# Softmax row sums over DMAs in place of VectorE turns, and a second pair of blocks joined, in a four-layer graph network on one core

## The chip, the core and the metric

The kernel runs on one core of a Trainium2 chip. The metric is the device time of one execution in microseconds, lower is better. The core has five engines that run their own instruction streams in order: TensorE (PE; its weight loads are PEld), VectorE (DVE), ScalarE (ACT), GpSimd (POOL) and SyncE (SP), which here only issues DMAs.

## What is computed

The input x holds 32 batches of 512 nodes with 64 features, adj is one 512 x 512 matrix. Each of four layers normalises x over its features, applies relu, and adds what a graph layer makes of it. Layers 0 to 2 take the first fifth of the time (the first `top_row` of layer 3 is issued at 464.4 us), and the change doesn't touch them. Layer 3, which the change is in, is a graph attention with eight heads and an output layer that is an attention of the same kind:

```
def gat_layer(x, graph, W, b):
    h = x @ W
    s = jnp.einsum('bnd,bmd->bnm', h, h) * graph
    s = jnp.where(s == 0.0, NEG_INF, s)
    a = jax.nn.softmax(s, axis=2)
    return jnp.einsum('bnm,bmd->bnd', a, h) + b
heads = jax.vmap(lambda W, b: gat_layer(flow_x, graph, W, b))(Wh, bh)
H, B, N, D = heads.shape
cat = jnp.moveaxis(heads, 0, 2).reshape(B, N, H * D)
x = jax.nn.leaky_relu(cat, negative_slope=0.01)
out = gat_layer(x, graph, W_out, b_out)
return jax.nn.leaky_relu(out, negative_slope=0.01)
```

So for each batch and head there is a 512 x 512 table of scores, an exp of it less the row's maximum, a sum of each row, a product of the exps with the values, and a division of that product by the row sums. All of it is fp32.

## The kernel before

**Units.** Layer 3 is cut into 144 units. A unit is a pair of attentions: two heads of one batch (class Heads, four units a batch), or the output layer of two batches (class Out). N = 512 is cut into C = 4 blocks of 128 rows (r, or j in the products), and a tile of a unit holds one block for both members of the pair, 128 x 1024. After eight units of heads comes one of Out, so the work repeats every nine units. Out follows the heads that it needs at a distance (LATE, line 305).

**The steps of a unit, by name and line (of the kernel before).**
- scores(r), L368: two matmuls into a PSUM tile `s_ps` of the pool `ps_s`, which has two buffers of two banks each.
- maxima(r), L380: VectorE reads `s_ps`, adds the mask, writes `p_att` to SBUF and leaves the row's extreme in `top`, once for each member of the pair.
- spread_out, L387 and L390: VectorE turns `top` in 32 x 32 blocks into `top_t`, and four DMAs write it to DRAM. spread_in, L396: one DMA reads it back, repeated over all 128 partitions, as `topb`.
- shift(r), L402: GpSimd subtracts `topb` from `p_att`.
- exps(r), L411: ScalarE's exp, in place; for r = 2 it goes to PSUM instead, into a tile `e_ps` that takes a buffer of `ps_s`.
- join, L414: VectorE adds block 1 to the `e_ps` of block 2 and writes the sum where block 2 was. Block 1 itself stays.
- totals, L435 and L443: TensorE sums over partitions with a matrix of ones into four groups of 32 rows of `tot_ps`: block 0 and the joined block over all 512 columns, and then block 3 in two halves of 256 columns. Then VectorE turns `tot_ps` (L450), and ScalarE gathers the first column of each block in five small copies (L453, L455) into `parts`.
- values(j), L422: the product with the values, in `av`, a PSUM tile with one buffer. Since the joined block holds e1 + e2 and is multiplied by v2, block 1 is multiplied by v1 - v2 (`hd` of L514, `gD` of L618), so that e1 v1 + e2 v2 comes out.
- recips, L461, L464 and L466: add the parts, take the reciprocal, turn it back over all partitions (`recb`).
- normalize, L473: `o_att` = `av` times `recb`.
- y_pe, y_act, y_dve (L555, L565, L573): the bias and leaky relu of heads, in `cat`. product (L601): the output layer's product with `wo_sb`, for odd batches. For Out: back, back_dve, back_pool and store.
- g (L537, copied by L549), hx (L298) and `gV` (L614) prepare later units.

**Their order.** No scheduler reorders this stage: the function planned writes out one period by hand, and each engine runs its instructions in the order in which they stand there. unit(k) in period t is the unit that began k periods ago, so one period works on units at different steps. Before the change, a unit has its scores and maxima 0 and 1 in period -1, 2 and 3 and the spread in period 0, the shifts, exps and the join in period 1, totals, values, recips and normalize in period 2, and y or back in period 3. VectorE's order in a period is: maxima 2 and 3, `top_t`, cat, maxima 0 and 1 of the next unit, `tot_t`, join, recips, normalize. SyncE's order is `top_row`, `topb` and, after an Out, the two stores of `out_dram`.

## Time and profile before

| | us |
|---|---|
| runs of the kernel before, median of 3 | 2138.51 |
| their lowest and highest | 2137.26, 2145.68 |
| the profiled execution | 2142.56 |
| its span, first to last instruction | 2140.8 |
| TensorE's granted clock in it | 0.986 of full speed |
| maxima on VectorE (L380), 1152 of them | 724.5 |
| shifts on GpSimd (L402), 576 | 1348.7 |
| turns of the totals (L450), 144 | 102.2 |
| small copies of `parts` (L455), 576 | 124.1 |

A group of the profile is one line, engine and form: its count, the busy time of all of them, the mean of one in nanoseconds, and then the idle time of its engine just ahead of it with what ended that. A timeline line is start, duration, engine, line, operation, output and inputs; where several instructions follow each other they are merged and their number stands last, and the idle time before them is in brackets. A window line is a stretch of the span, its length, and how long each engine was busy in it. Busy times of neighbours overlap a little[...], so where a length matters it is read from start to start.

### The profile page before, as it was taken

The numbers are of one execution on the slowest core, as the hardware profiler recorded it, in microseconds if no ns is written. First come the engines' busy times: TensorE is split into PE (matmuls) and PEld (weight loads), VectorE is DVE, ScalarE is ACT, GpSimd is POOL, SyncE is SP. The second block draws the span as 40 slices with busy tenths as digits, with TensorE's granted clock in tenths as the row PEclk, the third lists the DMA queues.
The fourth block names the chain that finished last, engine by engine and source line by source line (L and its number), as shares of the span: only waits on it lengthen the run. The fifth ranks groups of instructions, "written<-read, shape, count | busy, mean of one in ns | idle before, by whom it ended". The sixth has DMA issues, their size and how long they took to land.

```text
span 2140.8 us, 34626 instructions
## 1 busy us (share of the span) xinstructions
PE 2056.7 (96%) x12190; PEld 841.5 (39%) x12190; DVE 1825.7 (85%) x4401; ACT 1293.7 (60%) x2520; POOL 1428.5 (67%) x697
## 2 busy tenths in 40 slices
PE   7999999989999999999999999999999999999996
PEld 4667676643333333333333333333333333333332
DVE  6699997669888989898889889888988898888994
ACT  3444443337666767676666666766666676766654
POOL 3000000028888878888888888888887887878896
PEclk9999999979999999999999999999999999999998
DMA  5000000001111111111111111111111111111112
GB/s 137 1 1 1 1 2 1 2 21 50 41 50 54 42 55 51 45 50 55 41 55 55 41 55 51 45 50 55 41 55 50 41 50 41 50 50 42 49 50 52
DMA packets 54567, 89.90 MB, mean 42 GB/s; under 512 B 30008, under 2 KB 35296, under 8 KB 54256
## 3 DMA queue, kind: packets, MB, share of 16 engines
q1 hardware_dynamic: 53872, 87.39, 12.5%
q8 instruction: 98, 1.61, 0.3%
q0 software_dynamic: 512, 0.20, 0.1%
q14 instruction: 85, 0.70, 0.1%
HBM read 81.73 MB, written 4.78 MB: 40 GB/s over the span
## 4 chain that ended last, share of the span: by engine, by line
PE 61%; DVE 22%; ACT 7%; POOL 4%; issue 3%; DMA 3%; SPq 0%; DVEq 0%; POOLq 0%; ACTq 0%
PE av L422 17%; DVE p_att L380 13%; PE s_ps L368 9%; PE nt_ps L876 8%; PE acc L968 6%; PE gT_ps L601 5%; PE tot_ps L435 5%; POOL p_att L402 4%; PE g_ps L537 3%; DVE cat L573 2%; PE tot_ps L443 2%; DMA topb<-top_row 2%; ACT parts L455 1%; PE po L895 1%; ACT p_att L411 1%
## 5 line engine op out<-in xcount | busy, mean ns | idle before, releaser
L402 POOL TENSOR_TENSOR p_att<-p_att,topb 128x1024 f32<-128x1024 f32 x576 | 1348.7, 2376 | 280.7 <-DMA topb<-top_row 114.8
L380 DVE CUSTOM_DVE_ANT_0 p_att<-s_ps,flow_neg 128x512 f32<-128x512 f32 x1152 | 724.5, 684 | 120.6 <-PE s_ps L368 120.2
L368 PE MATMUL s_ps<-hx,g 64*128 64x512 f32 x2048 | 529.9, 615 | 25.7 <-DVE p_att L414 6.9
L411 ACT ACTIVATE p_att<-p_att 128x1024 f32<-128x1024 f32 x432 | 456.5, 1057 | 97.5 <-POOL p_att L402 89.4
L422 PE MATMUL av<-p_att,hn 128*64 128x512 f32 x1536 | 379.5, 601 | 0.0
L368 PEld LDWEIGHTS s_ps<-hx,g 64*128 64x128 f32 x2048 | 174.3, 186 | 334.3 <-DVE top L380 189.0
L411 ACT ACTIVATE e_ps<-p_att 128x1024 f32<-128x1024 f32 x144 | 148.0, 1028 | 172.5 <-DVE top L380 124.9
L1044 POOL TENSOR_TENSOR x<-x,bias_b 128x512 f32<-128x512 f32 x16 | 20.3, 1273 | 283.4 <-DVE hn L818 283.4
L573 DVE SCALAR_TENSOR_TENSOR cat<-y_ps,bh,cat 128x512 f32<-128x512 f32 x256 | 177.4, 734 | 16.9 <-ACT cat L565 13.0
L565 ACT ACTIVATE cat<-y_ps,bh 128x512 f32<-128x512 f32 x256 | 160.8, 679 | 33.0 <-PE y_ps L555 32.6
L414 DVE TENSOR_TENSOR p_att<-e_ps,p_att 128x1024 f32<-128x1024 f32 x144 | 170.7, 1185 | 7.5 <-ACT e_ps L411 7.5
L422 PEld LDWEIGHTS av<-p_att,hn 128*64 128x64 f32 x1536 | 98.8, 136 | 198.9 <-issue 198.9
L435 PE MATMUL tot_ps<-p_att,ones 128*32 128x512 f32 x1152 | 155.6, 612 | 10.4 <-DVE cat L573 9.5
L555 PE MATMUL y_ps<-o_att,wh_sb 64*128 64x512 f32 x512 | 133.3, 597 | 4.0 <-DVE o_att L473 4.0
L422 PE MATMUL av<-p_att,hd 128*64 128x512 f32 x512 | 131.6, 592 | 0.0
L455 ACT COPY parts<-tot_t 32x16 f32<-32x16 f32 x576 | 124.1, 215 | 6.7
L549 ACT COPY g<-g_ps 128x512 f32<-128x512 f32 x128 | 68.7, 589 | 95.7 <-PE g_ps L537 95.7
L968 PE MATMUL acc<-v,s 64*128 64x65 f32 x2048 | 123.8, 279 | 0.7 <-DVE s L954 0.4
L968 PEld LDWEIGHTS acc<-v,s 64*128 64x128 f32 x2048 | 120.8, 194 | 5.9 <-DVE o L984 1.2
L601 PE MATMUL gT_ps<-cat,wo_sb 128*64 128x512 f32 x512 | 120.7, 592 | 0.0
L876 PE MATMUL nt_ps<-adj_t,hn 128*128 128x512 f32 x256 | 119.2, 610 | 0.8 <-DVE hn L840 0.8
L450 DVE STREAM_TRANSPOSE tot_t<-tot_ps 128x512 f32<-128x512 f32 x144 | 102.2, 710 | 19.1 <-PE tot_ps L443 19.0
(186 smaller groups left out, 2291.8 us busy)
## 6 DMA issues: line engine op xcount, KB each, us to landing
topb<-top_row SPq DMA_DIRECT2D x144, 512.0 KB
top_row<-top_t SPq DMA_DIRECT2D x576, 1.0 KB
out_dram<-y SPq DMA_DIRECT2D x32, 128.0 KB
x<-in_x_dram SPq DMA_DIRECT2D x3, 1024.0 KB
x<-in_x_dram SPq DMA_DIRECT2D x4, 256.0 KB
adj_raw<-in_adj_dram SPq DMA_DIRECT2D x1, 1024.0 KB
mask<-mask SPq DMA_DIRECT2D x4, 256.0 KB
wh_sb<-in_L_gnn_Wh_dram SPq DMA_DIRECT2D x2, 256.0 KB
```

The lines of the kernel that those rows point to most:

```text
L368: nc.tensor.matmul(ps[:, k], lhsT=g[halves(k), r * P : (r + 1) * P], rhs=x[halves(k), :], start=True, stop=True,)
L380: nc.vector.tensor_tensor_reduce(out=self.p[r][:, k], in0=ps[:, k], in1=flow_neg[:, r], scale=-1.0, scalar=BIG, op0=OP.add, op1=OP.min, ac ...
L402: nc.gpsimd.tensor_tensor(self.p[r], self.p[r], self.topb, OP.subtract)
L411: nc.scalar.activation(to, self.p[r], AF.Exp, scale=-1.0)
L414: nc.vector.tensor_tensor(self.p[JOIN + 1], self.joined, self.p[JOIN], OP.add)
L422: nc.tensor.matmul(self.av[halves(k), :], lhsT=self.less_next(k) if j == JOIN else self.v(k, j), rhs=self.p[j][:, k], start=(j == 0), stop ...
L435: nc.tensor.matmul(ps[q : q + 32, :], lhsT=ones, rhs=self.p[j][:, k], start=True, stop=False,)
L565: nc.scalar.activation(self.cat[:, k], self.y[k], AF.Identity, bias=bh01[:, h : h + 1], scale=0.01)
L573: nc.vector.scalar_tensor_tensor(self.cat[:, k], self.y[k], bh[:, h : h + 1], self.cat[:, k], op0=OP.add, op1=OP.max,)
L601: nc.tensor.matmul(self.gps[halves(k), :], lhsT=wo_sb[:, h, :], rhs=Heads.cat.pop((self.b + k, h)), start=(h == 0), stop=(h == H - 1),)
L876: nc.tensor.matmul(p, lhsT=lhs(k), rhs=adj_t[:, k, :], start=(k == 0), stop=(k == C - 1))
L968: nc.tensor.matmul(self.acc[k][:, r], lhsT=self.s[b // 2][halves(k), b % 2, r * P : (r + 1) * P], rhs=self.v[halves(k), b], start=(b == 0) ...
```

## The change

It does four things, all in layer 3.

1. exps(1) and exps(3) go to PSUM (`e_ps`), in place of exps(2) alone; join(1) and join(3) add block 0 to 1 and block 2 to 3. Blocks 0 and 2 are multiplied by differences of values, so `hd` and `gD` hold two blocks each in place of one.
2. With two joined blocks the totals are four matmuls of 512 columns; the four of 256 columns are gone.
3. The turns and the small copies go. ScalarE copies `tot_ps` to SBUF, two DMAs lay the sums out 8 to a partition (`parts`), VectorE adds and inverts 8 columns in place of 16, one DMA writes the reciprocals to DRAM (`rec_row`), and two DMAs read them back, repeated over 64 partitions each (`recb`).
4. The division comes a period later: recips_in opens the next period, normalize follows cat there, ahead of the next unit's maxima 0 and 1, and y, back, store and the products are a period later too. LATE and ROOM grow by one. The shifts go in the order 0, 2, 1, 3.

```diff
         def exps(self, r):
             to = self.p[r]
-            if r == JOIN + 1:
+            if r % 2:
                 to = self.joined = ps_s.tile([P, 2, N], F32, name="e_ps", tag="s")
             nc.scalar.activation(to, self.p[r], AF.Exp, scale=-1.0)

-        def join(self):
-            nc.vector.tensor_tensor(
-                self.p[JOIN + 1], self.joined, self.p[JOIN], OP.add
-            )
+        def join(self, r):
+            nc.vector.tensor_tensor(self.p[r], self.joined, self.p[r - 1], OP.add)
...
         def totals(self):
             ps = ps_m.tile([P, N], F32, name="tot_ps", tag="m")
-            first, last = [j for j in range(C) if j not in (JOIN, JOIN + 1)]
-            for e, j in enumerate((first, JOIN + 1)):
+            for e in range(2):
                 for k in range(2):
                     q = (2 * k + e) * 32
                     nc.tensor.matmul(
-                        ps[q : q + 32, :], lhsT=ones, rhs=self.p[j][:, k],
-                        start=True, stop=False,
+                        ps[q : q + 32, :], lhsT=ones, rhs=self.p[2 * e + 1][:, k],
+                        start=True, stop=True,
                     )
+            self.tot = wk.tile([P, N], F32, name="tot", bufs=1)
+            nc.scalar.copy(self.tot, ps)
+
+        def totals_out(self):
+
+            self.parts = tiny.tile([P, 2, 8], F32, name="parts")
+            rows = self.tot.rearrange("(k e r) n -> k e r n", k=2, e=2)
             for e in range(2):
-                some = slice(e * N // 2, (e + 1) * N // 2)
-                for k in range(2):
-                    q = (2 * k + e) * 32
-                    nc.tensor.matmul(
-                        ps[q : q + 32, some], lhsT=ones, rhs=self.p[last][:, k, some],
-                        start=False, stop=True,
-                    )
...
+                nc.sync.dma_start(
+                    self.parts[:, e], rows[:, e, 0].rearrange("k (g i) -> k g i", i=8)
+                )

         def recips(self):
-            rec = tiny.tile([P, N // 32], F32, name="rec_flow")
+            self.rec = tiny.tile([P, 8], F32, name="rec_flow")
             nc.vector.tensor_reduce(
-                rec, self.parts.rearrange("p e b -> p b e"), AX.X, OP.add
+                self.rec, self.parts.rearrange("p e i -> p i e"), AX.X, OP.add
             )
-            nc.vector.reciprocal(rec, rec)
+            nc.vector.reciprocal(self.rec, self.rec)
+
+        def recips_out(self):
+            self.rec_row = dram.tile([2, N], F32, name="rec_row")
+            nc.sync.dma_start(
+                self.rec_row.rearrange("k (g i) -> (k g) i", i=8), self.rec
+            )
+
+        def recips_in(self):
             self.recb = wk.tile([P, N], F32, name="recb")
...
+            for k in range(2):
+                nc.sync.dma_start(
+                    self.recb[halves(k), :], self.rec_row[k : k + 1, :].to_broadcast([F, N])
+                )
...
             for r in range(2, C):
                 now.scores(r)
-            unit(3).y_pe()
+            unit(3).recips_in()
+            unit(4).y_pe()
             unit(1).shift(0)
             unit(1).exps(0)
-            unit(3).y_act()
+            unit(4).y_act()
...
-            unit(1).shift(1)
-            unit(1).exps(1)
+            unit(1).shift(2)
+            unit(1).exps(2)
...
-            unit(3).y_dve()
+            unit(4).y_dve()
+            unit(3).normalize()
             for r in range(2):
                 ahead.maxima(r)
             unit(-3).features(3)
-            unit(3).back()
-            unit(1).shift(2)
-            unit(1).exps(2)
-            unit(4).back_pool()
+            unit(4).back()
+            unit(5).back_pool()
             unit(-2).make_gs()
-            unit(4).store()
+            unit(5).store()
             unit(2).totals()
-            unit(1).shift(3)
-            unit(1).exps(3)
+            unit(2).totals_out()
+            unit(1).shift(1)
+            unit(1).exps(1)
             for j in range(C):
                 unit(2).values(j)
...
-            unit(1).join()
+            unit(1).join(1)
+            unit(1).shift(3)
+            unit(1).exps(3)
             unit(2).recips()
-            unit(3).back_dve()
-            unit(2).normalize()
+            unit(2).recips_out()
+            unit(4).back_dve()
+            unit(1).join(3)
             unit(1).make_v()
```

In the kernel after, L367 is scores, L379 maxima, L386 `top_t`, L389 `top_row`, L395 `topb`, L401 shift, L410 exps, L413 join, L419 values, L431 totals, L436 the copy of the totals, L443 `parts`, L449 and L452 recips, L456 `rec_row`, L463 `recb`, L469 normalize.

More of the change, by code (lines that the diff above doesn't have):

```diff
@@ L301, in pair_transpose @@
         return t
-    JOIN = 1
-    LATE = 5
-    ROOM = 5
+    LATE = 6
+    ROOM = 6
     tops = [const.tile([P, 32], F32, name=f"top{i}") for i in range(2)]
@@ L423, in values @@
                     self.av[halves(k), :],
-                    lhsT=self.less_next(k) if j == JOIN else self.v(k, j),
+                    lhsT=self.v(k, j) if j % 2 else self.less_next(k, j),
                     rhs=self.p[j][:, k],
@@ L449, in totals @@
-            turned = wk.tile([P, N], F32, name="tot_t", bufs=1)
-            nc.vector.transpose(turned, ps)
-            one = turned.rearrange("p (b j) -> p b j", j=32)[:, :, 0]
-            self.parts = tiny.tile([P, 2, N // 32], F32, name="parts")
-            nc.scalar.copy(self.parts[:, 0], one)
-            for q in range(Q):
-                nc.scalar.copy(
-                    self.parts[q * 32 : (q + 1) * 32, 1], one[(q ^ 1) * 32 : ((q ^ 1) + 1) * 32]
+                        ps[q : q + 32, :], lhsT=ones, rhs=self.p[2 * e + 1][:, k],
@@ L465, in recips @@
+        def recips_in(self):
             self.recb = wk.tile([P, N], F32, name="recb")
-            nc.vector.transpose(
-                self.recb.rearrange("p (b j) -> p b j", j=32),
-                rec[:, :, None].to_broadcast([P, N // 32, 32]),
-            )
+            for k in range(2):
+                nc.sync.dma_start(
+                    self.recb[halves(k), :], self.rec_row[k : k + 1, :].to_broadcast([F, N])
+                )
         def normalize(self):
@@ L512, in features @@
                     )
-                d = Heads.hd[b] = early.tile([P, F], F32, name="hd3", bufs=3)
-                nc.gpsimd.tensor_tensor(d, h[:, JOIN], h[:, JOIN + 1], OP.subtract)
+                d = Heads.hd[b] = early.tile([P, C // 2, F], F32, name="hd3", bufs=3)
+                nc.gpsimd.tensor_tensor(d, h[:, 0::2], h[:, 1::2], OP.subtract)
             else:
@@ L582, in v, with less_next @@
             return self.hnv[:, j, :]
-        def less_next(self, k):
-            return self.hdv
+        def less_next(self, k, j):
+            return self.hdv[:, j // 2]
     class Out(Pair):
@@ L616, in make_v @@
             nc.scalar.copy(self.gV, ps)
-            self.gD = wk.tile([P, P], F32, name="gD", bufs=1)
+            self.gD = wk.tile([P, C // 2, P], F32, name="gD", bufs=1)
             nc.vector.tensor_tensor(
-                self.gD, ps[:, JOIN], self.gV[:, JOIN + 1], OP.subtract
+                self.gD, ps[:, 0::2], self.gV[:, 1::2], OP.subtract
             )
@@ L634, in v, with less_next @@
             return self.gV[:, j, halves(k)]
-        def less_next(self, k):
-            return self.gD[:, halves(k)]
+        def less_next(self, k, j):
+            return self.gD[:, j // 2, halves(k)]
         def y_act(self):
@@ L777, in fast_form @@
             if b % 2:
-                products[len(flow) + 2] = out_unit, i
+                products[len(flow) + 3] = out_unit, i
             if due and len(flow) >= due[0][0]:
```

## Prediction, made before the change was run

> **What bounds the kernel now.** I read the page's busy shares first, then the busy times between one `top_t` (L387) and the next, which cuts layer 3 into its 144 periods, then each engine's timeline in one period, and SyncE's for the transfers.
>
> ```profile
> PE 2056.7 (96%) x12190; PEld 841.5 (39%) x12190; DVE 1825.7 (85%) x4401; ACT 1293.7 (60%) x2520; POOL 1428.5 (67%) x697
> ```
>
> ```profile
> 1297.98:1310.39 12.41, 12.35 (x64) 4.17 (x64) 10.05 (x25) 7.41 (x14) 9.67 (x5) 1.00 0.12 45
> 1321.26:1331.52 10.26, 10.09 (x53) 3.07 (x52) 9.97 (x26) 7.05 (x16) 9.03 (x5) 1.00 0.15 54
> ```
>
> Columns: length, then PE, PEld, DVE, ACT, POOL busy. The periods repeat every nine units (two batches, one output unit): 12.4, 10.4, 12.4, 12.2, 12.4, 10.9, 10.3, 10.7, 11.0, together 102.7 us, some 14.3 times. The long ones hold an output product (L601) and TensorE has no gap in them. In the short ones VectorE starts each instruction as the last one lets go:
>
> ```profile
> 1325.12 0.71 DVE L450 STREAM_TRANSPOSE tot_t<-tot_ps 128x512 f32<-128x512 f32 x1
> 1325.75 1.19 DVE L414 TENSOR_TENSOR p_att<-e_ps,p_att 128x1024 f32<-128x1024 f32 x1
> 1327.02 0.19 DVE L461 TENSOR_REDUCE rec_flow<-parts 128x16 f32<-128x32 f32 x1
> 1327.24 0.25 DVE L464 RECIPROCAL rec_flow<-rec_flow 128x16 f32<-128x16 f32 x1
> 1327.53 0.71 DVE L466 STREAM_TRANSPOSE recb<-rec_flow 128x512 f32<-128x512 f32 x1
> 1328.35 0.69 DVE L473 TENSOR_TENSOR o_att<-av,recb 128x512 f32<-128x512 f32 x1
> 1328.96 0.68 DVE L380 CUSTOM_DVE_ANT_0 p_att<-s_ps,flow_neg 128x512 f32<-128x512 f32 x1
> ```
>
> So two engines share the bound, and no transfer but `topb` is waited for. Its timing:
>
> ```profile
> 1250.77 1.28 SPq L390 DMA_DIRECT2D top_row<-top_t  x4
> 1252.98 0.34 SPq L396 DMA_DIRECT2D topb<-top_row  x1
> ```
>
> `topb` is issued 2.48 us after `top_t` starts (median). In the trace's packet records its 128 packets of 4 KB fill all 16 DMA engines; an engine is done with its share 2.4 to 3.3 us after the issue (median 2.7), and GpSimd starts on it 3.75 us after the issue.
>
> [...] the 8-row moves of `top_row` leave 8 packets and 8 four-byte writes each, `topb` (128 rows) leaves 16 writes.[...] output stores issued right after a `topb` (1276.72) move their first packet 1.8 us later, as it drains; without a `topb` ahead (issue at 2131.40) 1.1 us later.[...]
>
> **The change, part by part.** Let T be the start of a unit's maxima(2) on VectorE.
>
> *TensorE.* The sums lose the four 256-column matmuls (L443): the timeline has L435 at 1311.47, L443 at 1312.36, L422 at 1312.90, so 0.54 us of each period. A product period with g goes from 12.4 to 11.9.
>
> *VectorE.* Start to start, before: maxima 2.44 and 2.44, `top_t` 0.25, cat 1.28, `tot_t` 0.64, join 1.27, reduce 0.22, reciprocal 0.29, `recb` 0.81, division 0.61: 10.25, the short period. The change takes 1.45 (both turns) and adds a join of 1.20 and about 0.1 of wait of join(1) on its exp: that exp may start only when maxima(0) has freed the PSUM buffer (0.12 + 1.03 + 0.15 us, against 1.22 for maxima(1)). Reduce and reciprocal shrink by perhaps 0.05. Work: 10.0.
>
> *ScalarE.* Five small copies (1.12 us) for one of 128x512 (0.58, as L609); the exps into PSUM take 1028 ns for 1057. Hidden by its own slack (60% busy); without that cover it would be a gain of 0.6 us.
>
> *PSUM.* Six tiles a period now share the two score buffers, so scores(2) waits for join(1) and scores(3) for join(3). The first is early by 2 us. The second has VectorE's own maxima(2) as cover: 1.22 us against 0.86 + 0.21 for the scores and their hand-over (L368 to L380, 1.07 as at 1306.76 and 1307.83). Nothing, as long as join(3) isn't late.
>
> *Values wait for the division.* `av` has one buffer, and normalize of the unit ahead now comes after cat: T + 2.44 + 0.25 + 1.28 + 0.61 = T + 4.58. Then values (3.49), product (1.81), g (0.97) and the next scores with their hand-over (1.07) give 11.05 with a product, 12.02 with g too, 10.26 with g alone.
>
> *GpSimd.* Shift order only; the double `hd` costs under 0.4 us more once in four units. Unit n's chain over two periods (top_t 2.56, topb on GpSimd 6.24, four shifts 9.36, exp 1.3, join 1.2) needs two periods of 20.7: no bound where periods pass 10.4.
>
> *SyncE and the DMAs, where I see the cost.* Five new DMAs per unit: `parts` twice, `rec_row`, `recb` twice. The source of a `parts` DMA is two partitions (k) times 64 runs of 8 floats[...] two engines carry all 128 packets of 32 B, and both DMAs use the same two: 128 packets on each engine. They are written behind spread_in in SyncE's order, so they queue behind `topb`. The totals themselves are early (TensorE T + 3.6 to 4.5, the copy done at 5.3, issues over by about 6.8)[...]:
>
> - `top_t` at T + 2.56 (1260.37 to 1262.93), `topb` issued at T + 5.04, the engine free of it 2.70 later: T + 7.74.
> - 128 packets. No 32-byte row exists in this stage: a 128-byte packet occupies an engine 11 ns, and 256-byte ones follow each other every 21 ns (1024 packets on 16 engines in 1.35 us). I take 14 ns: 1.8 us (ends 1.4 and 2.7): T + 9.54.
> - VectorE sees it 0.41 later (`topb`'s last packet at 3.34 against GpSimd's start at 3.75): T + 9.95.
> - recips 0.45, join(3) 1.20, then the next maxima(2), whose scores are ready since join(1): a period of **11.6 us**; ends 10.9 (engine free at 2.4, 11 ns) and 13.1 (3.3, 21 ns).
>
> VectorE wants the parts at T + 8.37, so it stands 1.6 us in every period that TensorE doesn't hold. Queued behind this wait: join(3); behind that scores(3) on TensorE, which needs join(3)'s PSUM buffer, and with it y, values and all else there. recips_out and recips_in sit behind it on SyncE, and the next spread_out behind them.
>
> *The way back.* rec_row is seen 1.25 us after its issue (as `top_row`), two issues of `recb` (0.43 to 0.77 us each, the range of SyncE's plain loads), first packet after 0.97, some 0.4 to move, 0.41 to be seen: about 3.9 us after recips. The division comes 1.20 + 3.97 = 5.2 after them: hidden, with 1.3 to spare.
>
> *Sum over nine periods* at 11.6: 11.6 + 0.28 (gD, L618) = 11.9; product 11.6 twice; product and g 12.0; the period without y, 11.6 + 0.57 (back_dve ahead of join(3)) = 12.2; product, g and the stores, whose 64 packets per engine stand before `parts` (1.35), 12.95; three more at 11.6: 107.0 against 102.7. That is +4.3 times 14.3 = +61. The seven periods at the start go from 10.8 to 11.6 (+6); six output units at the end from 11.7 to 11.6 + 0.57 + 0.28 + 1.35 = 13.8 (+13); the tail loses turns and copies and gains two round trips (+4, an estimate). Together +84 on the profiled execution, 2142.56 (span 2140.8): 2226.5. It lies 4 us above the median of the runs, so **2222**.
>
> **The rivals.**
> - *B, faster: the parts spread over 16 engines, or pass `topb`.* Then they land near T + 8.4, are seen at 8.8, and the limit is 10.45: periods of 10.8, 11.05, 12.0, 11.0, 12.35, 11.05, 10.7, 10.5, 10.5 = 99.9, so -2.8 times 14.3 and +4 at the tail: 2102. For it: TensorE's 0.54 us is certain, and the destination has 128 rows. Against: the source's two rows[...]. It decides at a chain of 11.0, parts seen by T + 9.4.
> - *C, no change*: two engines, but 11 ns a packet and free early, chain 10.9 to 11.1: about 2140.
> - *D, slower by another wait: the way back is late.* The division, and so values and the next scores, wait for `recb`. It takes over once that leg passes 5.2 us. At 6.2 with the chain of A each period gains 1.0: 2222 + 144 = 2366. Against it: the 1.3 us of slack.
>
> **How the numbers follow.** A 0.68, B 0.20, C 0.05, D 0.07. A's own range is 2150 to 2330 (chains 11.0 to 12.3; at 12.3 the nine periods sum to 113, +178). The range 2100 to 2330 leaves out half of B, D and A's far end. A measurement here tells about 0.5% from no change: slower 0.74, within 0.06, faster 0.20.
>
> **What would show it.** Right: VectorE idle before the smaller reduce (L449), released by the `parts` DMA, about 1.6 us in most periods; TensorE's wait before scores for VectorE's join; short periods near 11.6 and nearly equal to the product ones; 32-byte packets on two engines after `topb`. Wrong: the reduce starts at once after the join and product periods shrink to 12.0 (B); or the idle time lies before L469 and is released by `recb` (D).

## The result and the profile after

The changed kernel takes 2157.4 us (median of 4 runs, 2155.88 to 2158.13) against 2139.94 us for the kernel before on the same chip: a ratio of 1.0077, with a 95% interval of 1.0055 to 1.0099. It is slower, as forecast, but by 17 us in place of 83. The profiled execution took 2158.13 us, its span is 2156.3.

The busy shares of the page after, and the first line of its chain of waits (share of the span by engine), after and before:

```profile
PE 2004.3 (93%) x11038; PEld 836.9 (39%) x11038; DVE 1787.3 (83%) x4257; ACT 1224.3 (57%) x1944; POOL 1430.5 (66%) x697
```

```profile
PE 50%; DVE 21%; DMA 11%; POOL 6%; ACT 5%; issue 3%; SPq 3%; POOLq 0%; DVEq 0%; ACTq 0%
```

```profile
PE 61%; DVE 22%; ACT 7%; POOL 4%; issue 3%; DMA 3%; SPq 0%; DVEq 0%; POOLq 0%; ACTq 0%
```

TensorE lost 1152 matmuls and 52 us of work, VectorE 38 us, and the kernel got longer: no engine is busier than it was by more than 2 us (GpSimd), so the time has gone into waits. In the chain of the kernel before, DMAs had 3% and PE 61%; now they have 11%, PE has 50%, and SyncE's queue 3%. TensorE's granted clock doesn't explain it: from 660 to 1930 us it is 1.00 in both traces.

Four periods of the kernel after, from one `top_t` to the next (columns: length, busy time of PE, PEld, DVE, ACT, POOL): one with a product and g, one with a product, one in which gs is made, one with g and gV.

```profile
1307.10:1319.37 12.27, 12.04 (x58) 4.27 (x56) 9.88 (x24) 7.24 (x11) 11.42 (x7) 1.00 0.31 87
1319.37:1330.66 11.29, 11.13 (x52) 3.82 (x52) 9.82 (x24) 7.09 (x13) 8.59 (x4) 1.00 0.22 65
1330.66:1342.44 11.78, 9.43 (x44) 3.10 (x44) 10.39 (x26) 7.02 (x12) 10.83 (x6) 1.00 0.23 77
1259.76:1272.56 12.80, 12.00 (x54) 4.03 (x52) 10.11 (x26) 8.92 (x17) 11.29 (x6) 1.00 0.25 71
```

In the first two TensorE is still busy almost throughout. The third has TensorE busy for 9.4 of 11.8 us, VectorE for 10.4 and GpSimd for 10.8: nobody is full, and before the change the periods that held gs were short ones (10.86 us). The fourth is the longest, and TensorE is busy for 12.0 of its 12.8 us.

Where layer 3 went, by the start of every unit's `top_t` in the two traces (us):

| | before | after | difference |
|---|---|---|---|
| start to unit 0 (layers 0 to 2, not touched) | 464.1 | 460.6 | -3.5 |
| units 0 to 17 | 189.6 | 193.8 | +4.2 |
| units 17 to 89, eight cycles of nine | 827.0 | 838.6 | +11.6 |
| units 89 to 128, nearly all heads | 448.4 | 442.3 | -6.1 |
| units 128 to 143, with the last output units | 172.3 | 177.4 | +5.1 |
| the tail | 39.5 | 43.6 | +4.1 |

The first row lies between 458 and 464 us in all traces of this study, so a few us of it are chance. The rest tells that cycles of nine became longer (103.4 to 104.8 us), and that heads without output units became *shorter* (92.0 to 90.7 us for eight). In the last two rows a part may be the clock: from 1930 to 2090 us it is 1.00 before and 0.98 after.

The way of the sums in one period of the kernel after (start, duration; `top_t` starts the period, `x2` are two issues):

```profile
1319.37 0.21 DVE L386 STREAM_TRANSPOSE top_t<-top 128x32 f32<-128x32 f32 x1
...
1321.63 0.58 ACT L436 COPY tot<-tot_ps 128x512 f32<-128x512 f32 x1 [0.91 <-ACT p_att L410]
...
1322.02 0.35 SPq L395 DMA_DIRECT2D topb<-top_row  x1
...
1322.42 1.17 SPq L443 DMA_DIRECT2D parts<-tot  x2
...
1325.82 0.17 DVE L449 TENSOR_REDUCE rec_flow<-parts 128x8 f32<-128x16 f32 x1 [0.76 <-DMA parts<-tot]
...
1326.03 0.20 DVE L452 RECIPROCAL rec_flow<-rec_flow 128x8 f32<-128x8 f32 x1
1326.24 1.22 DVE L413 TENSOR_TENSOR p_att<-e_ps,p_att 128x1024 f32<-128x1024 f32 x1
```

VectorE stands for `parts`, as forecast, but for 0.76 us. Over the whole span, the waits with their sum, count and longest:

```profile
PEld s_ps L367 <- DVE p_att L413: 142.0, 129, 9.1
...
DVE rec_flow L449 <- DMA parts<-tot: 91.9, 107, 3.6
...
PE av L419 <- DVE o_att L469: 26.6, 75, 1.8
...
DVE o_att L469 <- DMA recb<-rec_row: 18.3, 18, 4.7
```

The stand is 0.86 us in 107 of 144 units. Scores wait for the joins (L413), as forecast; the way back (last line) is hidden in 126 of 144.

Two waits were not in the forecast, both at output units. In the period with g and gV, the turned values hold one of the two buffers of their PSUM pool, so the two halves of g have to share the other: the second starts only when ScalarE has copied the first (1267.33 to 1267.91), where without gV both are issued in one go. The scores behind it are late, and VectorE stands 1.98 us before its maxima:

```profile
1265.59 0.66 PE L610 MATMUL gV_ps<-ident,gT 128*128 128x128 f32 x4
...
1267.33 0.58 ACT L545 COPY g<-g_ps 128x512 f32<-128x512 f32 x1 [0.47 <-PE g_ps L533]
...
1267.97 0.69 PE L533 MATMUL g_ps<-hx,m 64*128 64x512 f32 x1 [0.68 <-ACT g L545]
...
1269.99 0.69 DVE L379 CUSTOM_DVE_ANT_0 p_att<-s_ps,flow_neg 128x512 f32<-128x512 f32 x1 [1.98 <-PE s_ps L367]
```

In the period with gs, GpSimd stands for ScalarE's copy of the transposed product (gT) and then makes gs, with shift(1) and shift(3) behind it. (Before, three shifts stood ahead of gs in place of two, and GpSimd waited for the copy 0.4 us at most in these nine periods of the cycles, 0.5 to 1.9 now.) Both joins are late, and the scores with them:

```profile
1331.61 1.29 POOL L620 TENSOR_TENSOR gs<-gT,urow 128x512 f32<-128x512 f32 x1 [0.99 <-ACT gT L605]
...
1337.61 1.13 PE L367 MATMUL s_ps<-hx,g 64*128 64x512 f32 x4 [1.04 <-DVE p_att L413]
...
1338.64 1.22 DVE L413 TENSOR_TENSOR p_att<-e_ps,p_att 128x1024 f32<-128x1024 f32 x1 [0.77 <-ACT e_ps L410]
...
1339.92 1.13 PE L367 MATMUL s_ps<-hx,g 64*128 64x512 f32 x4 [1.18 <-DVE p_att L413]
```

Theory 1: what is lost, is lost in two places: VectorE's stand for `parts` in most units, and these two collisions of the output units. Rival: one of the two is hidden by the other or by TensorE, and doesn't cost.

### The profile page after: what moved, and what is told of

It is laid out like the page before. It is cut to its first block, busy times and chain, and to the rows that moved or that the text cites. A ratio compares the mean times of both kernels' runs of the same rounds, so it can differ in the third digit from the quotient of the medians.

```text
span 2156.3 us, 32793 instructions
## 1 busy us (share of the span) xinstructions
PE 2004.3 (93%) x11038; PEld 836.9 (39%) x11038; DVE 1787.3 (83%) x4257; ACT 1224.3 (57%) x1944; POOL 1430.5 (66%) x697
## 4 chain that ended last, share of the span: by engine, by line
PE 50%; DVE 21%; DMA 11%; POOL 6%; ACT 5%; issue 3%; SPq 3%; POOLq 0%; DVEq 0%; ACTq 0%
PE av L419 14%; DVE p_att L379 11%; PE nt_ps L876 7%; PE s_ps L367 7%; PE acc L968 6%; POOL p_att L401 5%; DMA parts<-tot 4%; PE gT_ps L597 4%; PE g_ps L533 3%; DVE cat L569 3%; DVE p_att L413 3%; DMA topb<-top_row 2%; PE tot_ps L431 2%; DMA recb<-rec_row 2%; DVE o_att L469 2%
## 5 line engine op out<-in xcount | busy, mean ns | idle before, releaser
L401 POOL TENSOR_TENSOR p_att<-p_att,topb 128x1024 f32<-128x1024 f32 x576 | 1346.1, 2369 | 285.0 <-DMA topb<-top_row 148.9
L379 DVE CUSTOM_DVE_ANT_0 p_att<-s_ps,flow_neg 128x512 f32<-128x512 f32 x1152 | 728.6, 685 | 94.4 <-PE s_ps L367 93.2
L367 PE MATMUL s_ps<-hx,g 64*128 64x512 f32 x2048 | 542.2, 618 | 62.8 <-DVE p_att L413 50.1
L410 ACT ACTIVATE e_ps<-p_att 128x1024 f32<-128x1024 f32 x288 | 295.4, 1028 | 187.6 <-DVE top L379 89.8
L410 ACT ACTIVATE p_att<-p_att 128x1024 f32<-128x1024 f32 x288 | 304.2, 1056 | 140.1 <-POOL p_att L401 139.0
L413 DVE TENSOR_TENSOR p_att<-e_ps,p_att 128x1024 f32<-128x1024 f32 x288 | 346.4, 1203 | 35.9 <-ACT e_ps L410 35.2
L367 PEld LDWEIGHTS s_ps<-hx,g 64*128 64x128 f32 x2048 | 176.3, 186 | 371.7 <-DVE top L379 141.8
L419 PE MATMUL av<-p_att,hd 128*64 128x512 f32 x1024 | 272.7, 602 | 28.8 <-DVE o_att L469 24.8
L419 PE MATMUL av<-p_att,hn 128*64 128x512 f32 x1024 | 269.3, 592 | 0.0
L569 DVE SCALAR_TENSOR_TENSOR cat<-y_ps,bh,cat 128x512 f32<-128x512 f32 x256 | 178.4, 738 | 11.3 <-ACT cat L561 8.5
L431 PE MATMUL tot_ps<-p_att,ones 128*32 128x512 f32 x1152 | 154.3, 608 | 3.0 <-DVE cat L569 2.5
L419 PEld LDWEIGHTS av<-p_att,hd 128*64 128x64 f32 x1024 | 71.3, 136 | 208.0 <-issue 96.8
L551 PE MATMUL y_ps<-o_att,wh_sb 64*128 64x512 f32 x512 | 142.4, 604 | 0.0
L419 PEld LDWEIGHTS av<-p_att,hn 128*64 128x64 f32 x1024 | 85.8, 137 | 133.9 <-issue 133.9
L436 ACT COPY tot<-tot_ps 128x512 f32<-128x512 f32 x144 | 84.3, 585 | 85.1 <-ACT p_att L410 45.6
```

The source lines that it names most:

```text
L367: nc.tensor.matmul(ps[:, k], lhsT=g[halves(k), r * P : (r + 1) * P], rhs=x[halves(k), :], start=True, stop=True,)
L379: nc.vector.tensor_tensor_reduce(out=self.p[r][:, k], in0=ps[:, k], in1=flow_neg[:, r], scale=-1.0, scalar=BIG, op0=OP.add, op1=OP.min, ac ...
L401: nc.gpsimd.tensor_tensor(self.p[r], self.p[r], self.topb, OP.subtract)
L410: nc.scalar.activation(to, self.p[r], AF.Exp, scale=-1.0)
L413: nc.vector.tensor_tensor(self.p[r], self.joined, self.p[r - 1], OP.add)
L419: nc.tensor.matmul(self.av[halves(k), :], lhsT=self.v(k, j) if j % 2 else self.less_next(k, j), rhs=self.p[j][:, k], start=(j == 0), stop= ...
```

## The experiments

Every ratio below is to the kernel before on the same chip, with its 95% interval. The kernel after is at 1.0077 on that scale.

**The output units: gV last, gs last, both.** In period(), make_v moved behind make_hx and make_g; make_gs moved behind shift(3). (make_gs also holds a reduction of gT on VectorE, 0.68 us, which moves with it. It held nothing up: in the kernel after, join(1) stands behind it and still waits 0.52 to 0.76 us for its exponential in all nine such periods of the cycles.)

```diff
-            unit(1).make_v()
             unit(-3).make_hx()
             unit(-2).make_g()
+            unit(1).make_v()
```

```diff
-            unit(-2).make_gs()
...
             unit(1).shift(3)
+            unit(-2).make_gs()
             unit(1).exps(3)
```

> The kernel after, with make_v moved behind make_hx and make_g on every engine, so that the PSUM buffer of gV, which VectorE gives back only after join(3), is no longer the one that the second g matmul needs. Theory 1 (the loss sits in two collisions of the output units, this one and gs): the period with gV goes from 12.8 to 13.7 us to about 11, nine times, so about 18 us faster than the kernel after: 2139. Rival (the parts leg is what costs in every period, the output units only show it): within 4 us of the kernel after, 2157.

Measured: 2147.94 us, 1.0045 [1.0029, 1.0061].

> The kernel after, with make_gs moved behind shift(3), so that GpSimd no longer stands before shift(1) and shift(3) for ScalarE's copy of gT. Theory 1: the period with gs goes from 11.8 to about 10.7, nine times in the cycles and a little at the end: 10 to 15 us faster than the kernel after, 2144. Rival (parts leg): within 4 us, 2157.

Measured: 2142.08 us, 1.0024 [1.0014, 1.0034].

> Both moves of the two kernels before this one. Theory 1: the two gains add, 28 us: 2129, faster than the kernel before the change by 0.5%. Rival (parts leg): 2150 or more.

Measured: 2134.07 us, 0.9986 [0.9976, 0.9996].

The collisions are real and cost 0.9%, about 20 us, more than the kernel lost. The gains of each alone (0.32% and 0.53%) sum to 0.85%. (Where an expectation names `gD` as what frees the buffer, the timeline above corrects it: it is the copy of g.) The first gave half of what I expected. The period with g and gV fell from 13.1 to 12.2 us and not to 11, because now gV waits for g's copy in the same buffers (0.67 us in each of the nine). And the gs period grew from 11.9 to 12.5, so that in the trace of this kernel the eight cycles take 838.3 us, as long as in the kernel after: with this collision cured alone, its gain in the cycles is taken by the other.

**The stand for `parts`.** The two DMAs left out, the reduce reads a constant tile (`some_parts`, made once).

```diff
-            self.parts = tiny.tile([P, 2, 8], F32, name="parts")
-            rows = self.tot.rearrange("(k e r) n -> k e r n", k=2, e=2)
-            for e in range(2):
-                nc.sync.dma_start(
-                    self.parts[:, e], rows[:, e, 0].rearrange("k (g i) -> k g i", i=8)
-                )
+            self.parts = some_parts
```

> The kernel after, with the two parts DMAs left out: recips reads a constant tile, so the division is by a constant and not by the row sums. Everything else, the way back by rec_row and recb too, is there. Theory 1: the wait for parts is 74 us in the stretch from 600 to 2000 us, but much of it lies in periods that TensorE bounds; only the short periods shorten, from 10.5 to 10.1, some 60 times: 15 to 30 us faster than the kernel after, 2135. Rival (parts leg is the whole cost): faster by 50 us or more, 2105.

Measured: 2133.63 us, 0.9983 [0.9973, 0.9992]. The two DMAs and the stand for them cost 0.94%, some 20 us, against the 92 us that the waits list: units 17 to 89 fell from 838.6 to 829.2, units 128 to 143 from 177.4 to 171.9, the tail from 43.6 to 40.2. (SyncE is also free of the two issues, 1.16 us a unit; what share of the gain is theirs isn't separated.) In the stretch of heads alone nothing changed (442.3 to 442.0), although the stand is there too (15.6 us of it between 1640 and 2000 us). What limits it is seen in this kernel's timeline (its L404, L413 and L416 are shift, exp and join):

```profile
1851.09 1.03 ACT L413 ACTIVATE e_ps<-p_att 128x1024 f32<-128x1024 f32 x1 [0.80 <-POOL p_att L404]
...
1851.90 9.34 POOL L404 TENSOR_TENSOR p_att<-p_att,topb 128x1024 f32<-128x1024 f32 x4 [0.43 <-DVE rec_flow L450]
...
1852.15 1.23 DVE L416 TENSOR_TENSOR p_att<-e_ps,p_att 128x1024 f32<-128x1024 f32 x1 [0.29 <-ACT e_ps L413]
```

ScalarE waits for the fourth shift, join(3) for ScalarE. (The second line names `rec_flow`; it lies 3.63 us after the issue of `topb` at 1848.27, so it is `topb` that GpSimd waits for.) That is the chain over two periods, 20.7 us, which I put down as "no bound where periods pass 10.4". The periods of this stretch without a product mostly take 10.4 to 10.7 us in the kernel after and 10.4 to 10.6 here; three get down to 9.96 to 10.2, and the product period behind each of these is longer (12.5 to 13.6 us in place of 12.3).

**Both cures:** gV and gs last, and the two DMAs left out.

> The changed kernel with the turn of the output unit's values and the scaling of its product placed behind the other work, and with the two transfers of the sums left out: the reciprocals read a constant tile, so that the output isn't divided by the right sums. Theory (two separate losses, in different periods): the gains of each alone, 23 and 24 us of 2157, add up, to 2108 to 2116 us. Rival (one hides the other): no more than 8 us below the better of the two, 2126 to 2134 us.

Measured: 2110.55 us, 0.9885 [0.9868, 0.9901]. From the kernel after it is 1.9%, the sum of 0.91 and 0.94 within the noise: two separate losses. Theory 1 holds.

**Recips behind join(3)**, so that join(3) doesn't stand for `parts`.

```diff
-            unit(2).recips()
-            unit(2).recips_out()
             unit(4).back_dve()
             unit(1).join(3)
+            unit(2).recips()
+            unit(2).recips_out()
```

> The changed kernel with the reciprocals (and the transfer of their result to memory) moved behind the second join on VectorE's queue. Theory: what the two transfers of the sums cost is that VectorE stands for them ahead of join(3), so with join(3) ahead the cost goes as it did with the transfers left out (2133.6 us, a ratio of 0.998 to the kernel before): 2130 to 2142 us, VectorE's idle time on the sums' parts under a third of the 92 us it was, and the way back still hidden since it had time to spare: idle time on the broadcast reciprocals under 20 us. Rival: the whole leg of DMAs has no room, the later reciprocals come back too late for the division, VectorE waits for the broadcast in most units (over 60 us in all), and the time stays at 2150 us or above.

Measured: 2190.03 us, 1.0251 [1.0232, 1.0270]. My theory fell, the rival held. The stand for `parts` is gone from the list's top, and in its place is "DVE o_att L469 <- DMA recb<-rec_row", 68.6 us in 66 units. In one such period:

```profile
1253.03 1.15 SPq L463 DMA_DIRECT2D recb<-rec_row  x2
...
1254.53 1.76 SPq L389 DMA_DIRECT2D top_row<-top_t  x4
...
1257.01 0.69 DVE L469 TENSOR_TENSOR o_att<-av,recb 128x512 f32<-128x512 f32 x1 [1.49 <-DMA recb<-rec_row]
...
1257.72 0.35 SPq L395 DMA_DIRECT2D topb<-top_row  x1
```

SyncE holds at L463 for `rec_row`, and `top_row` of the next unit stands behind it: `topb` leaves 3.70 us after `top_t` (1254.02) where 2.56 is usual, and GpSimd waits 2.60 us for it; it leaves later than 2.9 us in 46 units, where the kernel after has 19. So the 1.3 us that the way back had to spare are all that it had: the sums' round trip is tight at both ends.

**Spread over 16 engines**: four DMAs of one source row each.

```diff
             for e in range(2):
-                nc.sync.dma_start(
-                    self.parts[:, e], rows[:, e, 0].rearrange("k (g i) -> k g i", i=8)
-                )
+                for k in range(2):
+                    nc.sync.dma_start(
+                        self.parts[halves(k), e],
+                        rows[k : k + 1, e, 0].rearrange("k (g i) -> k g i", i=8),
+                    )
```

> The changed kernel with the sums' parts in four transfers of one source row each, in place of two of two rows: the 256 packets spread over all 16 DMA engines in place of two. Theory (what VectorE waits for is the place behind the broadcast of the minima and the two issues, not the packets, which all moved in 0.75 us): at most 0.6 us a unit is gained in flight and two more issues of 0.58 us on SP are lost, so VectorE's idle time on the parts stays at 90 us or grows, and the time is 2150 to 2175 us. Rival (the step of the forecast: packets on two engines are what takes the time): the wait falls under 30 us, and the time under 2140 us.

Measured: 2212.01 us, 1.0354 [1.0340, 1.0367]; the wait on the parts is 209.8 us. The packet records have 16 semaphore writes for each of these DMAs, where each of the two had 2, which I read as the spread. The last issue ends 5.48 us after `top_t` in place of 4.19 (medians), and the reduce starts at 7.18 in place of 6.44: the two more issues cost more than the spread gives. The rival, my forecast's own step, is not borne out, but it isn't excluded either: on two engines the packets start within 0.78 us, 0.78 of the 6.44 us, and that much is nearly the whole stand of 0.86. What a spread without more issues would save stays open.

**Issued from ScalarE's queue**, right behind the copy of the sums, alone and with both output units' cures; then one of the two DMAs from each queue, with the cures.

```diff
-                nc.sync.dma_start(
+                nc.scalar.dma_start(
                     self.parts[:, e], rows[:, e, 0].rearrange("k (g i) -> k g i", i=8)
                 )
```

```diff
-                nc.sync.dma_start(
+                (nc.sync, nc.scalar)[e].dma_start(
```

> The changed kernel with the parts' two transfers issued from ScalarE's queue, straight behind the copy of the sums, in place of SP's, where they stood behind the broadcast of the minima. Theory (the wait is the place in SP's queue[...]): VectorE's idle time on the parts falls from 92 us to under 20, and the time goes to 2130 to 2140 us, as with the parts' transfers left out (2133.6). Rival: ScalarE stands about 1.2 us for the two issues ahead of the exponentials into PSUM, the joins come that much later, and the time is 2150 us or more.

Measured: 2157.30 us, 1.0109 [1.0091, 1.0127]. The theory was right on VectorE's wait (19.7 us) and wrong on the time: the wait has only moved. The sums hardly come earlier (their last packet starts 5.91 us after `top_t` in place of 6.00, medians); it is VectorE that comes to them later. ScalarE stands 1.2 us for the two issues (1309.32 to 1310.38 in one period, behind the end of the copy at 1309.29 and ahead of the exp at 1310.49, which join(1) needs). The list of waits puts it down to the DMA:

```profile
ACT e_ps L410 <- DMA parts<-tot: 147.3, 122, 1.8
```

> The changed kernel with all three cures: the turn of the output unit's values and the scaling of its product placed behind the other work (2134.1 us alone), and the parts' transfers issued from ScalarE's queue. Theory (the two causes, output units and the wait for the parts, lie in different periods and add up): 2108 to 2120 us, faster than the kernel before by about 1%. Rival (they share the same periods, the wait for the parts only takes the place of the others): 2128 to 2140 us.

Measured: 2137.26 us, 1.0001 [0.9991, 1.0010]. By its number the rival won, but it is the same stand on ScalarE (154.8 us), not a shared period; the run without the DMAs, above, is the one that tells.

> The changed kernel with the output units' work moved behind the other work (2134.1 us), and of the sums' two transfers one issued from SP's queue and one from ScalarE's, so that the two issues of 0.58 us run beside each other. Theory (the way of the sums is tight by the issue): VectorE's idle time on the parts falls from 91 us to 40 to 60, ScalarE stands 0.6 us a unit in place of 1.2 and hides it, and the time is 2118 to 2128 us. Rival (the place behind the minima's broadcast[...] holds the first transfer as before, and ScalarE's stand is paid in addition): 2133 to 2142 us.

Measured: 2127.36 us, 0.9958 [0.9943, 0.9972], the fastest kernel here that does all the work, and faster than both. But not for the reason given: the wait on the parts fell only to 65.1 us. The issues are over 0.54 us earlier than with the cures alone (3.64 us after `top_t` in place of 4.18), and where VectorE waits, the reduce starts 6.37 us after `top_t` in place of 6.43. One unit:

```profile
1320.16 0.50 ACTq L443 DMA_DIRECT2D parts<-tot  x1
1320.18 0.35 SPq L395 DMA_DIRECT2D topb<-top_row  x1
...
1320.63 0.57 SPq L443 DMA_DIRECT2D parts<-tot  x1
...
1323.82 0.17 DVE L449 TENSOR_REDUCE rec_flow<-parts 128x8 f32<-128x16 f32 x1 [0.71 <-DMA parts<-tot]
```

In the packet records `topb`'s packets start from 1321.14 to 1323.10, the 128 of ScalarE's queue from 1322.65 to 1323.03 and the 128 of SyncE's from 1323.03 to 1323.41: one after the other, and both behind `topb`'s first ones. Over all units the reduce starts 0.08 us earlier than with the cures alone (6.35 for 6.42), with fewer waits (97 for 110). Times 144 that is 11 us, an estimate from these two medians, and more than the 6.7 us gained; that the gain comes from there is not shown.

**An output unit seven places behind** (LATE = 7, with gs last), so that gV meets no g.

> The changed kernel with an output unit seven places behind in place of six, so that the turn of its values falls in a period in which no next output unit's product is begun, and with GpSimd's scaling of the product placed behind the fourth shift. Theory: the two waits of the output units go (the second matmul group of g for the PSUM buffer of gV, and the shifts for the copy of the transposed product), each some 1 to 1.5 us of a cycle of nine units: 2122 to 2132 us, under the 2134.1 us that moving both behind the others gave, since there the turned values still wait for g's copy. Rival: the collisions only move to other periods, as when one of the two was moved alone, and it is no better than 2134 us.

Measured: 2141.15 us, 1.0018 [1.0008, 1.0027]: worse than both moved (2134.07). The rival held: the period that held g and gV and now holds g alone fell to 10.6 us, and the product period that now holds gV rose from 11.3 to 12.3.

**The division ahead of cat**, with both output units' cures.

> The changed kernel with the output units' work moved behind the other work (2134.1 us), and with the division ahead of the two additions to the concatenated heads on VectorE, 1.4 us earlier. Theory (the way back has 1.3 us to spare at most, and the sums' PSUM buffer comes free 0.7 us later): VectorE waits for the broadcast reciprocals in the short periods, the wait on them grows from 16 us to over 50, the sums start later, and the time is the same or worse, 2134 to 2150 us. Rival (the division's place is what holds the value products, and nothing else): the product periods lose 0.3 us each, and the time is 2118 to 2128 us.

Measured: 2208.04 us, 1.0356 [1.0333, 1.0378]: the theory's direction, and worse than its number. The wait on `recb` grew to 73.5 us, and the larger part is the other one: cat holds the PSUM buffer that the sums need, and it is 0.7 us later. TensorE's wait for it was 2.5 us in the kernel after, and is here

```profile
PE tot_ps L431 <- DVE cat L569: 117.5, 128, 2.6
```

So TensorE's wait for the division can't be had back by moving the division ahead of cat.

**The parts of the change alone.** First the second join with the turns kept: in the kernel before, both exps into PSUM, both joins, the sums of two blocks, differences of two; the division stays in its own unit and join(3) comes last on VectorE. Then the same with join(3) ahead of the division, and with the exp for join(1) ahead of the sums and of the copies of the parts on ScalarE. (The expectation says this of both exps; the one for join(3) stands behind the copies, in the code and in the trace.)

```diff
-            unit(1).join()
+            unit(1).join(1)
+            unit(1).shift(3)
+            unit(1).exps(3)
             unit(2).recips()
             unit(3).back_dve()
             unit(2).normalize()
+            unit(1).join(3)
```

> The kernel before with the second join alone: two of the four exponentials go into PSUM, VectorE adds both pairs, two blocks of sums go; the sums are still turned on VectorE (two transposes and the copies), and the division stays in its own unit. Theory: VectorE has 1.2 us more in every period and TensorE 0.5 less, VectorE becomes the bound where it was not: about 11.4 us in the periods without a product and about 12.4 in those with one, some 2200 us, over 2% slower than the kernel before; so the DMAs are what pays for the join. Rival: VectorE's addition hides in the gaps it had, and the time is within 0.7% of the kernel before (2125 to 2153 us).

Measured: 2618.60 us, 1.2257 [1.2233, 1.2282]. Neither held. VectorE isn't full here (77%); "PEld s_ps L367 <- DVE p_att L413" is 578.1 us in 261 waits. With join(3) behind a division that waits for the values, and scores behind join(3), the engines take turns. TensorE's granted clock is 0.89 from 660 to 2500 us as well, where it is 1.00 in the kernels before and after up to 1930 us; why isn't shown, and what part of the time it takes isn't separated. It prices an order, not the join.

> The kernel before with the second join and without the DMAs, in a better order than the run with the joins alone: both exponentials into PSUM come before the copies of the parts can hold ScalarE, and join(3) stands ahead of the division on VectorE. Theory: with the chain through the division gone, VectorE's own work sets the pace, at 11.4 us and more in every period: 2190 to 2260 us. Rival: an order was all that was amiss, the second addition fits into VectorE's gaps, and the time is 2125 to 2153 us, so that the DMAs were needless.

Measured: 2172.07 us, 1.0163 [1.0150, 1.0176], below the range that I gave and well above the rival's. The same kernel once more, for its profile:

> A look at the kernel before with both joins and the turns, in the better order (2172 us). Theory: VectorE starts each instruction as the last one ends in the periods without a product, 11.4 us and more of work, and those periods are about 11.4 us where they were 10.3 to 10.9. Rival: VectorE has gaps there, and waits for the parts' copies or the division set the pace.

```profile
PE 2026.1 (93%) x11038; PEld 805.5 (37%) x11038; DVE 1972.5 (91%) x4545; ACT 1296.2 (60%) x2520; POOL 1432.0 (66%) x697
```

This one run took 2178.32 us. VectorE at 91% has taken over the bound: in the stretch of heads alone the periods are mostly 11.2 to 12.0 us, where they were 10.5 to 12.4, and the plain ones over the whole layer have a median of 11.46, as the theory had it. Not all of the loss is VectorE's: the nine periods of the cycles that hold gs take 12.7 us (median) where they took 10.9. But the product periods with g are 11.98 us, down from 12.41: TensorE has its saving in full, 0.43 us (the sums take 0.45 us less), where values don't wait for the division.

Then the transfers with one join as before, once with its exp ahead of the copy of the sums on ScalarE and once behind it.

> The changed kernel with one join, as before: one exponential of four goes into PSUM, TensorE adds the sums of three blocks; the reciprocals over DMAs, the division a unit later and an output unit six places behind stay. Theory: VectorE has 1.45 us less in each period, GpSimd's fourth shift is not behind an addition that TensorE waits for, so the short periods go under 10.3 us, those with products stay on TensorE: 2110 to 2135 us, faster than the kernel before. Rival: the wait for the parts' transfers holds VectorE with one join as well, nothing is gained from the turns, and the time is the kernel before's or more, 2140 to 2155 us.

Measured: 2207.24 us, 1.0342 [1.0320, 1.0365]. The rival's side, and beyond it: the wait on the parts is 257.3 us, in all 144 units. ScalarE's exp into PSUM waits for maxima to free the buffer (303.6 us in all), the copy of the sums stands behind it, and the issues end 6.43 us after `top_t` in place of 4.19 (medians). So this, too, prices an order.

> The changed kernel with one join, and with the exponential into PSUM placed behind the copy of the sums and their transfers, as the changed kernel has it; three blocks of sums, one difference of values. Theory (VectorE's second addition fills time in which it would stand for the parts, which land 6.4 us after the turn of the maxima whatever it does): the wait on the parts is about as in the changed kernel plus part of the addition, 90 to 200 us in all, the product periods have TensorE's 0.54 us back and are 12.4 us again, and the time is 2130 to 2150 us, no better than the kernel before by more than 0.4%. Rival (the second addition is what costs, the transfers alone are a gain): 2105 to 2125 us.

Measured: 2146.18 us, 1.0047 [1.0028, 1.0066]. The theory held for the time and for the product periods with g, which are 12.4 us again, and not for the wait: on the parts VectorE stands 76.4 us, below the 90 to 200 that I gave and less than in the kernel after (91.9). It has 163 us less to do than there, and most of that time it now stands for scores. The two lines, here and in the kernel after:

```profile
DVE p_att L380 <- PE s_ps L368: 239.3, 129, 3.5
```

```profile
DVE p_att L379 <- PE s_ps L367: 93.2, 82, 2.7
```

The time is 0.3% better, a difference that is hardly clear of the noise (each ratio has some 0.2% on either side).

Together: the join alone in a good order is +1.6%, the transfers alone +0.5%, both +0.8%. With the transfers the second join costs 0.3% in place of 1.6%: with the turns gone VectorE has room for it, and without it stands 146 us longer for scores.

## Why the prediction was right in sign and wrong in size

- *TensorE's 0.54 us.* The sums took 218.6 us before and take 154.3 now, 0.45 us a unit, and of that only a part came. Product periods with g are 12.2 to 12.4 us at their two places in the cycle (forecast 12.0), with a product alone 11.3 to 11.4 (forecast 11.05): values wait for the division (1.35 us from the start of the sums to that of the values, 1962.10 to 1963.45), as the forecast said, and these periods are 0.2 to 0.4 us longer than I worked out. By the terms that the forecast lists the gap is 0.1 us wider still: they add up to 10.95, 11.92 and 10.11 us, where it has 11.05, 12.02 and 10.26.
- *VectorE's turns and joins.* Right: 1825.7 us before, 1787.3 after, and a join takes 1203 ns.
- *PSUM.* Join(1) and join(3) hold scores as described; "nothing, as long as join(3) isn't late" needed its condition: in the periods with gs, scores wait 1.0 to 1.3 us for join(1) and 1.2 us for join(3).
- *The leg of the parts: the step that failed.* Term by term, in medians of the kernel after: `topb` issued 2.56 us after `top_t` (forecast 2.48), the engine free of it, by the first 32-byte packet, 2.61 us after that issue (2.70), **all 256 packets in 0.78 us where I had 1.8**, seen 0.42 us later (0.41). The whole leg is 6.44 us after `top_t` (its median; the medians of the terms add up to 6.37), T + 9.0 in place of T + 9.95. I took 14 ns a packet from wide packets that follow each other at 21 ns; 0.78 us over 128 on each engine is 6 ns. The mechanism was right: behind `topb`, and in two interleaved sequences of starts (6 ns from one to the next but one, the median of all units), which I read as two engines. For the forecast two engines were an assumption; nothing that it reads from the kernel before shows them for a source of two rows. A stand of 1.6 us became 0.86. Rival C (two engines, quick packets) named this term, and stopped at 11 ns a packet; its 2140 us lacks the collisions that follow here. (One reading of the forecast is a little off, and no sum uses it: the store issued at 2131.40 moves its first 256-byte packet 1.2 us later, not 1.1.)
- *With that term mended*, rival B's point is passed (parts seen by T + 9.4), and by the same sum the nine periods are 12.0, 11.2, 12.0, 11.05, 10.6, 10.6, 10.6, 10.9 and 11.05, together 100.0: the kernel should have been faster. Measured is 12.2, 11.1, 12.4, 11.4, 11.9, 10.9, 10.6, 13.1 and 11.3, together 104.8. Of the 4.8 us that are missing, 1.3 are the gs period, 2.2 the period with g and gV, and most of the rest the product periods. This is the second step that failed, and a term that I put at nothing without a reason: I had gone through the queues for the parts and not for make_gs and make_v, although the change touches both. The two have different causes. LATE = 6 puts gV into a period with g; before, with LATE = 5, the nine periods of the cycles that hold gV have no g and take 11.0 us (median). gs stays in the period of the copy that it needs; it is the second join, with the new order of the shifts, that puts two joins behind it: in the kernel with both joins and LATE = 5 (the joins in the better order, above) these nine periods take 12.7 us, and in the one with one join and LATE = 6 (the last run above) 9.9, although gs waits there too (0.7 to 1.7 us). With both steps moved and the parts left out, the cycles take 101.1 us, near that sum: lines of the change that I read as bookkeeping cost as much as its DMAs.
- *GpSimd.* The chain of 20.7 us over two periods was put down as no bound, since periods were to pass 10.4. Where no output unit interferes they don't pass it by much: the periods without a product come down to about 10.4 us and stay there, also without the parts. The second join doesn't lengthen its shifts: 2335 to 2412 ns each after the change, 2347 to 2428 before.
- *The way back hidden, with 1.3 us to spare* was right, and the spare was real: moving the reciprocals behind one join used it up.
- *The sum.* I multiplied by 14.3 cycles of nine. The output units stand in the flow only up to about unit 89; then come some 39 units of heads, in which the change gains 6.1 us, and the last output units at the end (+5.1, forecast +13). The tail was +4.1 (forecast +4).

The direction came out for half of the reason: without the parts' DMAs alone (0.9983), or without the collisions alone (0.9986), the kernel is 0.1 to 0.2% faster than before. That the sign came out right is luck in that sense: of two losses of about 20 us each, one was forecast much larger and the other not seen, and with either one alone the sign would have been wrong.

## What to carry to other kernels

When a change shifts a software pipeline by a period, list for every step that moves the PSUM buffer it needs and the instruction that frees it; and when it puts more work behind a step in an engine's queue, ask what that step itself waits for. Do both for the rare steps too: two of them cost 20 us here. A round trip through DMAs has to be laid out end by end: here the way back had 1.3 us to spare where the way out lacked 0.9, and reciprocals placed behind one more join (1.2 us) turned the first into a wait, and two more issues (1.3 us) lengthened the second. If no packet of the size is in the trace, bound its price as far below as above: here 14 ns was taken, 11 was the low end, and 6 came.

## What the runs showed of the hardware

- 256 packets of 32 bytes from SBUF to SBUF, 128 on each of two DMA engines, all start within 0.78 us (median of the 144 units of the kernel after): about 6 ns apart on an engine, where a record says that one took 9 ns (the median). The records don't name the engine; that it is two I read from the starts, which make two interleaved sequences, 6 ns from one to the next but one (median), and from the kernel that issues from ScalarE: its queue leaves 576 four-byte semaphore writes for 288 DMAs, two each.
- Here a second queue did not pass a transfer in flight. With `topb` under way, the first 32-byte packet starts 2.17 us after its issue from SyncE's queue and 2.21 from ScalarE's (medians), both 2.5 to 2.6 us after `topb`'s issue; with `topb` already drained (the transfers alone, issued 2.6 us after `topb`) it is 1.20. With one of the two DMAs from each queue, the issues are over 0.54 us earlier and the reduce that takes the sums starts 0.08 us earlier than with both from SyncE's; the packets of the two halves came one queue after the other (in the unit above, 1322.65 to 1323.03 and 1323.03 to 1323.41). My forecast had put the wait down to SyncE's queue alone.
- One such issue takes 0.53 to 0.58 us on SyncE and 0.50 to 0.53 on ScalarE, where `topb`, of 512 KB, takes 0.35; on ScalarE two of them hold back the next exp for 1.20 us (median of 122 units).
- TensorE's granted clock was 0.89 from 660 to 2500 us in the kernel in which the engines took turns (TensorE busy for 82% of that stretch), and 1.00 from 660 to 1930 us before the change (98%) and after (95%).
